# Two resnorm layers on one core: the hand-made order of every engine written anew, step by step, with a table of places per group

## The chip, the cores and the metric

The kernel runs on one core of one Trainium2 chip. The metric is the device time of one execution in microseconds (us), the median of several runs. Five instruction streams matter: PE (TensorE, matrix products), DVE (VectorE), ACT (ScalarE), POOL (GpSimd) and SP (SyncE, which only issues DMA transfers). Each stream is executed strictly in the order in which it was written; between streams there are semaphores.

## The reference, cut to what matters

`x` is 128 samples of 128 nodes by 512 features in float32, `adj` a 128 by 128 matrix. Layer 0 adds a graph convolution's maximum to `x` and normalizes; layer 1 is masked self-attention with 8 heads, a projection, an inner normalization with gamma and beta, a residual and an outer normalization.

```
# layer 0: one number per node is added to its 512 features
A   = adj @ x[b];  r = max(relu(A + b0), over the features)
x1  = layernorm(x[b] + r)
# layer 1
q, k, v = x1 @ w_qkv                      # 8 heads of 64
attn = softmax(where(adj == 0, -inf, q @ k.T / 8))
o    = (attn @ v) @ w_proj + b_proj
out  = layernorm(x1 + o + layernorm(o) * gamma + beta)
```

## The kernel before

The 128 samples go in 32 groups of 4. A group passes through a software pipeline: its layer 0 is computed while the group before it makes its queries, keys and values, its softmax runs while the next group's layer 0 runs, and its projection overlaps the scores of the group after it.

The products with `w_qkv` and `w_proj` must be close to float32, but are run in the format float32r on parts with fewer bits. So each operand is split into a high part, a low part and a difference (`split`, `split_high`, `split_d`, lines 290 to 308), and each product is twelve 128x512 matmuls: eight into one PSUM bank (`product`, lines 342 and 343) and four into another (`product_d`, line 350). ACT takes the first bank out (`dense_main`), DVE adds the second (`dense_rest`). A group has 16 such products: 8 for queries and keys of all four samples (`dense` 4 to 11), 4 for values (`dense` 0 to 3), 4 for the projection (`po`). Besides them PE does, for each sample, the convolution (`conv`, line 186, 2 matmuls), the scores (`scores`, "S", line 397, 16 matmuls of 64x128) and the weighting of the values (`attend`, "AV", line 477, 16 matmuls of 128x64).

The transposes of the normalized `x` and of the attention weights are not made on PE but by DMA: ACT copies the two 16-bit halves of each number apart (`x_halves`, `halves`), a DMA writes them to DRAM (`rowsx`, `rows`), and a transposing DMA brings them back (`xT`, `eT`). Only in the last group are the weights transposed by PE ("T", line 464).

Buffers that matter: PSUM pool `ps_1` has four banks for one-bank tiles (convolution, AV, most products), `ps_2` two double banks (scores, some products); attention weights `e` have 3 buffers, their transposes `eT` 2, the projected `o` 3, the residual `xb` 2, `xt` 4.

The order of all streams is written by the program itself. Lines 561 to 872 make a list `plan` of (place, function): a PE order is fixed by hand (`pair_order`, `dense_order`, `tail_order`, `pro_order`), each PE step gets a place by adding lengths, and every other step is placed at a distance from its PE step, taken from the table `O`, within limits. The same distances hold for all groups; the first group has its own (`pro`), the last group and the one before it have partly their own (`final`, `last`, `tail`). Several instructions of one engine, or of two, are one step: `split` is two DVE instructions, `residual_x` two POOL ones, `stats` one ACT and three to four POOL ones, `halves` an ACT copy and a DMA, `norm_2` an ACT instruction and the DMA of the output. The sorted list is then run under `tc.manual_schedule`, so its order is the order on each engine, and only the order: the place itself is not a time that anything waits for. At the start `warm` (line 261) puts 28 small matmuls with no use into PE's stream.

Of the kernel before, what the change touches and what calls it, by code (L numbers as in the profile page):

```python
# [10 lines left out]
I32 = mybir.dt.int32  # L11
# [13 lines left out]

@with_exitstack
def tile_adj_resnorm_d2(
# [12 lines left out]

# [20 lines left out]
    xraws, rows, ends, xs, c0s, rms, pa, mv0s, pts, hs = {}, {}, {}, {}, {}, {}, {}, {}, {}, {}  # L85
    pps, qkTs, vs, pscs, es, ppts, eTs = {}, {}, {}, {}, {}, {}, {}
    pavs, oTs, xbs, os, sums_of, norms = {}, {}, {}, {}, {}, {}

    def load_x(b):
        xt = xpool.tile([P, D], FP, tag="xt", name=f"xt_{b}")  # L90
        nc.sync.dma_start(xt, x[b])
        xs[b] = xt


# [7 lines left out]
    adjT_ps = ps_1.tile([P, P], FP, tag="ps1", name="adjT_ps")  # L102
    nc.tensor.transpose(adjT_ps, adj_sb, ident)
    adjT = const.tile([P, P], FP, name="adjT")
    nc.vector.tensor_copy(adjT, adjT_ps)

    mask = const.tile([P, P], FP, name="mask")
    nc.vector.tensor_scalar(mask, adj_sb, 0.0, MASKED, op0=ALU.is_equal, op1=ALU.mult)
# [5 lines left out]

# [5 lines left out]
    raws = {}  # L120
# [15 lines left out]
    def load_w(c):  # L136
        if c < KC:
            if c % 2 == 0:
                pair = work.tile([P, 2, D], FP, tag="e", bufs=3, name=f"wraw_{c}")
                raws[c], raws[c + 1] = pair[:, 0, :], pair[:, 1, :]  # L140
            nc.scalar.dma_start(raws[c], part(c)[0])
            return
        raws[c] = work.tile([P, D], FP, tag="o", bufs=3, name=f"wraw_{c}")
        nc.sync.dma_start(shaped(c, raws[c]), part(c)[0])

    def split_w(c):

        _, (dst_h, dst_l, dst_d) = part(c)
        raw = raws.pop(c)
        wh = work.tile([P, D], FP, tag="xh", name=f"wh_{c}")  # L150
        nc.vector.tensor_scalar(wh.bitcast(I32), raw.bitcast(I32), HIGH, None, op0=ALU.bitwise_and)
        nc.vector.tensor_tensor(raw, raw, wh, op=ALU.subtract)
        nc.vector.scalar_tensor_tensor(
            dst_d, shaped(c, raw), HALF, shaped(c, wh), op0=ALU.mult, op1=ALU.subtract,
        )
        hs["w", c] = dst_h, dst_l, wh, raw

    def split_w_rest(c):
        dst_h, dst_l, wh, raw = hs.pop(("w", c))
        nc.scalar.activation(dst_h, shaped(c, wh), AF.Copy, scale=HALF)  # L160
        nc.scalar.activation(dst_l, shaped(c, raw), AF.Copy, scale=HALF)

    def row(vec):
        return bass.AP(tensor=vec.tensor, offset=vec.offset, ap=[[0, P], [1, D]])

    gamma_sb = const.tile([P, D], FP, name="gamma_sb")
    bias_sb = const.tile([P, D], FP, name="bias_sb")
    beta_sb = const.tile([P, D], FP, name="beta_sb")
    nc.vector.memset(mhalf, -0.5)
    square = const.tile([P, D], mybir.dt.bfloat16, name="square")  # L170

    nc.scalar.activation(mhalf, mhalf, AF.Copy)

    def load_gamma():
        nc.sync.dma_start(gamma_sb, row(ln_gamma))
        nc.sync.dma_start(bias_sb, row(b_proj))
        nc.sync.dma_start(beta_sb, row(ln_beta))


    def conv(b):  # L180

        g, i = divmod(b, G)
        if i == 0:
            rms[g] = small.tile([P, G], FP, tag="rm", bufs=2, name=f"rm_{g}")
        pa[b] = ps_1.tile([P, D], FP, tag="ps1", name=f"pa_{b}")
        nc.tensor.matmul(pa[b], adjT, xs[b], start=True, stop=True)  # L186

    def conv_max(b):
        g, i = divmod(b, G)
        nc.vector.tensor_reduce(rms[g][:, i : i + 1], pa.pop(b), AX.X, ALU.max)  # L190

    def relu_0(b, n):

        g, i = divmod(b, G)
        r = rms[g][:, i : i + n]
        nc.gpsimd.tensor_scalar(r, r, b0_sb, 0.0, op0=ALU.add, op1=ALU.max)

    def add_0(b):
        g, i = divmod(b, G)
        if g not in mv0s:  # L200
            mv0s[g] = small.tile([P, G, 4], FP, tag="sum0", bufs=5, name=f"sum0_{g}")
        nc.scalar.activation(
            xs[b], xs[b], AF.Identity, bias=rms[g][:, i : i + 1], accum_out=mv0s[g][:, i, 0:1],
        )

    def stats_0(b):
        g, i = divmod(b, G)
        squares(xs[b], mv0s[g][:, i, :])

    def rstd_0(b, n):  # L210
        g, i = divmod(b, G)
        total, ssq, nmean, shift = (mv0s[g][:, i : i + n, k] for k in range(4))
# [3 lines left out]
        for k in range(n):  # L216
            norms[b + k, 0] = ssq[:, k : k + 1], nmean[:, k : k + 1]
            c0s[b + k] = ssq[:, k : k + 1], shift[:, k : k + 1]

    def shift_0(b, n):  # L220

        g, i = divmod(b, G)
        _, ssq, nmean, shift = (mv0s[g][:, i : i + n, k] for k in range(4))
        nc.gpsimd.tensor_tensor(shift, rms[g][:, i : i + n], ssq, op=ALU.mult)
        nc.gpsimd.tensor_tensor(shift, shift, nmean, op=ALU.add)

    def stats_x(b):

        g, i = divmod(b, G)
        if g not in mv0s:  # L230
            mv0s[g] = small.tile([P, G, 4], FP, tag="sum0", bufs=5, name=f"sum0_{g}")
        st = small.tile([P, 6], FP, tag="bnst", bufs=2, name=f"bnst_{b}")
        nc.vector.bn_stats(st, xs[b])
        nc.vector.bn_aggr(mv0s[g][:, i, 0:2], st)

    def rstd_x(b, n):

        g, i = divmod(b, G)
        var = mv0s[g][:, i : i + n, 1]
# [3 lines left out]
    def shift_x(b, n):  # L243

        g, i = divmod(b, G)
        mean, rstd, both, shift = (mv0s[g][:, i : i + n, k] for k in range(4))
        r = rms[g][:, i : i + n]
# [3 lines left out]
        for k in range(n):  # L251
            norms[b + k, 0] = c0s[b + k] = rstd[:, k : k + 1], shift[:, k : k + 1]

    def norm_0(b, vector=False):
        rstd, nm = norms.pop((b, 0))
        if vector:
            nc.vector.tensor_scalar(xs[b], xs[b], rstd, nm, op0=ALU.mult, op1=ALU.add)
            return
        nc.scalar.activation(xs[b], xs[b], AF.Identity, bias=nm, scale=rstd)  # L259

    def warm(n):

        spare = ps_2.tile([P, 2, D], FP, tag="ps2", name=f"spare_{n}")
# [3 lines left out]
    def transpose_x(b):  # L267
        g, i = divmod(b, G)
        pts[b] = ps_1.tile([P, KC, P], FP, tag="ps1", name=f"ptx_{b}")
        xt = xs[b]  # L270
# [3 lines left out]
    def x_halves(b):  # L274

        planes = work.tile([P, 2, D], U16, tag="xplanes", bufs=1, name=f"xplanes_{b}")
        nc.scalar.copy(planes, xs.pop(b).bitcast(U16).rearrange("p (m s) -> p s m", s=2))  # L277
        rows["x", b] = dram.tile([P, 2, D], U16, tag="rowsx", bufs=8, name=f"rowsx_{b}")
        nc.sync.dma_start(rows["x", b], planes)

    def crossbar_x(b):
# [5 lines left out]

    x_forms = [group.tile([P, KC, G, P], FR, name=f"x_{n}") for n in "hld"]

    def split(key, src, dsts):  # L290

        _, fl, _ = dsts
        xh = work.tile([P, KC, P], FP, tag="xh", name=f"xh_{key}")
        nc.vector.tensor_scalar(xh.bitcast(I32), src.bitcast(I32), HIGH, None, op0=ALU.bitwise_and)  # L294
        hs[key] = dsts, xh
        nc.vector.tensor_tensor(fl, src, xh, op=ALU.subtract)  # L296

    def split_high(key, gpsimd=False):
        (fh, _, _), xh = hs[key]
        if gpsimd:  # L300
            nc.gpsimd.tensor_scalar(fh, xh, 1.0 / HALF, None, op0=ALU.mult)
        else:
            nc.scalar.activation(fh, xh, AF.Copy, scale=1.0 / HALF)

    def split_d(key, gpsimd=False):
        (fh, fl, fd), _ = hs.pop(key)
        engine = nc.gpsimd if gpsimd else nc.vector
        engine.tensor_tensor(fd, fh.bitcast(FP), fl.bitcast(FP), op=ALU.subtract)  # L308

    def copy_x(b, vector):  # L310

        xraws[b] = work.tile([P, H, P], FP, tag="eT", bufs=2, name=f"xraw_{b}")[:, :KC, :]
# [5 lines left out]
    def product_v(b):  # L318

        pps["v", b] = pv = ps_1.tile([P, D], FP, tag="ps1", name=f"pv_{b}")  # L320
        for kc in range(KC):
            nc.tensor.matmul(pv, xraws[b][:, kc, :], raws[kc], start=(kc == 0), stop=(kc == KC - 1))

    def keep_v(b):
        nc.scalar.copy(dense_to(0, b), pps.pop(("v", b)))

    def split_x(b):

        split(b, pts.pop(b), [f[:, :, b % G, :] for f in x_forms])


    def product(key, two, terms):

        if two:
            pp = ps_2.tile([P, 2, D], FP, tag="ps2", name=f"pp_{key}")
            pm, pd = pp[:, 0, :], pp[:, 1, :]
        else:
            pm = ps_1.tile([P, D], FP, tag="ps1", name=f"pm_{key}")
            pd = ps_1.tile([P, D], FP, tag="ps1", name=f"pd_{key}")
# [4 lines left out]
        pps[key] = pm, pd  # L344
        ends[key] = terms

    def product_d(key):
        terms, pd = ends.pop(key), pps[key][1]
# [3 lines left out]
    def dense(g, j, two):  # L352


        parts = [*zip(x_forms, qkv_forms)]
        if j < G:
            product((g, j), two, lambda kc: [(f[:, kc, j, :], w[:, kc, 2 * D :]) for f, w in parts])
            return
        c, k = divmod(j - G, 2)
        cs = slice(k * D + c * P, k * D + (c + 1) * P)  # L360
        product(
            (g, j), two,
# [536 lines left out]
```

## Time and profile before

| what | before |
|---|---|
| time, median of 3 runs | 1974.43 us (1974.4 to 1975.56) |
| profiled span | 1969.2 us |
| PE busy | 1844.8 us (94%) |
| DVE busy | 1671.3 us (85%) |
| ACT busy | 1550.6 us (79%) |
| POOL busy | 1273.3 us (65%) |
| DMA traffic | 302.92 MB, mean 154 GB/s |

"Busy" is the time in which an engine had an instruction in execution, as a share of the span. Line numbers (L397 and so on) are those of the kernel before. In a timeline a row gives the start, the duration, the engine and the operation, and in brackets the idle time before it with what ended it. A matmul's duration reaches past the start of the next one, since they are pipelined; the distance between two starts is what a matmul costs.

### The profile page before, as it was taken

The page shows a single profiled execution, that of the slowest core. Times are in us where ns is not written, and L with a number is a line of the kernel's source. Part 1 is how long each engine was busy: PE and PEld are TensorE (multiplying, and loading weights), DVE is VectorE, ACT ScalarE, POOL GpSimd, SP SyncE. Part 2 cuts the span into 40 slices and gives each one's busy share as a digit, 9 for nine tenths or more (in the row PEclk, how much of TensorE's full clock was granted, in tenths as well). Part 3 has the DMA queues.
Part 4 walks back from the last instruction along what each step waited for, and adds up shares of the span by engine and source line. Part 5 has one row for each costly group of instructions (what it writes and reads, how often), then busy time and mean ns, then how long its engine had stood idle before and what let it go on. Part 6 is the DMA issues. An engine that isn't in the chain of part 4 may idle for free.

```text
span 1969.2 us, 33044 instructions
## 1 busy us (share of the span) xinstructions
PE 1844.8 (94%) x10569; PEld 1438.0 (73%) x10569; DVE 1671.3 (85%) x2585; ACT 1550.6 (79%) x3926; POOL 1273.3 (65%) x1935
## 2 busy tenths in 40 slices
PE   7799999999999999999999999999999999999995
PEld 4677777777777777777777777777777777777774
DVE  7678888888888888888888888888888888888885
ACT  4688878788878788878788878788778788778764
POOL 3156667666667666667666667666667666667667
PEclk9899999999999999999999999999999999999997
DMA  4356565666565666555666555665555665555641
GB/s 130 102 156 165 152 160 146 171 171 168 150 160 148 169 171 166 150 159 148 170 171 168 150 159 147 166 174 158 154 161 145 174 172 159 155 161 145 155 114 53
DMA packets 486141, 302.92 MB, mean 154 GB/s; under 512 B 399440, under 2 KB 403664, under 8 KB 485968
## 3 DMA queue, kind: packets, MB, share of 16 engines
q1 hardware_dynamic: 485104, 299.70, 57.5%
q8 instruction: 84, 1.38, 0.3%
q10 hardware_dynamic: 864, 1.12, 0.2%
q14 instruction: 89, 0.73, 0.1%
HBM read 72.16 MB, written 131.07 MB: 103 GB/s over the span
## 4 chain that ended last, share of the span: by engine, by line
PE 59%; POOL 14%; DVE 9%; ACT 7%; issue 5%; DMA 5%; POOLq 0%; ACTq 0%; SPq 0%; DVEq 0%
POOL x_d L308 5%; PE pav L477 4%; PE psc L397 4%; DMA eT<-rows 3%; PE pa L186 2%; POOL od L308 2%; ACT e L431 2%; POOL sum L536 2%; POOL xb L501 1%; DVE x_l L296 1%; DVE v L381 1%; DVE xh L294 1%; POOL xb L518 1%; POOL xb L500 1%; DVE o L523 1%
## 5 line engine op out<-in xcount | busy, mean ns | idle before, releaser
L431 ACT ACTIVATE e<-e,nmax 128x128 f32<-128x128 f32 x1016 | 393.1, 389 | 61.6 <-DVE nmax L422 61.6
L446 ACT COPY planes<-e 128x2048 uint16<-128x2048 uint16 x124 | 235.0, 1895 | 24.1 <-DVE e L440 21.6
L535 POOL TENSOR_SCALAR sum<-sum 128x1 f32<-128x1 f32 (+1 forms) x287 | 57.7, 201 | 284.7 <-ACT square L529 271.6
L529 ACT ACTIVATE square<-o,sum 128x512 bf16<-128x512 f32 x256 | 183.0, 715 | 63.7 <-DVE o L523 62.6
L501 POOL TENSOR_TENSOR xb<-xb,beta_sb 128x512 f32<-128x512 f32 x128 | 210.5, 1645 | 10.7
L308 POOL TENSOR_TENSOR x_d<-x_h,x_l 128x512 fp32r<-128x512 f32 x97 | 125.5, 1308 | 110.2 <-DVE x_l L296 51.6
L536 POOL TENSOR_TENSOR sum<-sum,mhalf 128x1 f32<-128x1 f32 (+1 forms) x287 | 180.1, 628 | 23.9
L431 ACT ACTIVATION_READ_ACCUMULATOR e<-e,nmax 128x1 f32 x1016 | 191.4, 188 | 0.0
L518 POOL TENSOR_TENSOR xb<-xb,o 128x512 f32<-128x512 f32 x125 | 175.2, 1401 | 4.9
L477 PE MATMUL pav<-eT,v 128*64 128x128 f32 x2048 | 140.7, 280 | 37.3 <-DMA eT<-rows 28.7
L548 DVE SCALAR_TENSOR_TENSOR o<-o,sum,gamma_sb 128x512 f32<-128x512 f32 x128 | 99.3, 776 | 75.4 <-POOL xb L518 71.9
L440 DVE TENSOR_TENSOR e<-e,sums 128x1024 f32<-128x1024 f32 x128 | 157.7, 1232 | 4.4
L477 PEld LDWEIGHTS pav<-eT,v 128*64 128x64 f32 x2048 | 110.8, 137 | 63.5 <-ACT square L529 19.9
L413 DVE SCALAR_TENSOR_TENSOR e<-psc,mask 128x1024 f32<-128x1024 f32 x127 | 152.0, 1217 | 3.4 <-ACT planes L446 2.7
L422 DVE TENSOR_REDUCE nmax<-e 128x8 f32<-128x1024 f32 x127 | 153.6, 1210 | 0.1
L259 ACT ACTIVATE xt<-xt,sum 128x512 f32<-128x512 f32 x127 | 102.4, 806 | 57.7 <-POOL sum L250 56.7
L556 ACT ACTIVATE o<-o,sum 128x512 f32<-128x512 f32 x128 | 103.2, 807 | 54.4 <-POOL sum L544 54.4
L397 PE MATMUL psc<-qkT 64*128 64x128 f32 x2048 | 142.6, 285 | 2.9 <-DVE qkT L381 2.6
L500 POOL TENSOR_SCALAR xb<-xb,sum 128x512 f32<-128x512 f32 x128 | 120.8, 944 | 34.2 <-DMA xb<-in_x_dram 34.0
L397 PEld LDWEIGHTS psc<-qkT 64*128 64x128 f32 x2048 | 124.1, 190 | 25.8 <-issue 21.6
L523 DVE SCALAR_TENSOR_TENSOR o<-o,sum,xb 128x512 f32<-128x512 f32 x128 | 132.5, 1035 | 10.8 <-POOL sum L536 0.9
L277 ACT COPY xplanes<-xt 128x1024 uint16<-128x1024 uint16 x124 | 129.7, 1046 | 6.2 <-DMA rowsx<-xplanes 2.4
(4668 smaller groups left out, 5611.1 us busy)
## 6 DMA issues: line engine op xcount, KB each, us to landing
rows<-planes SPq DMA_DIRECT2D x124, 512.0 KB, 3.4
xt<-in_x_dram SPq DMA_DIRECT2D x128, 256.0 KB, 3.0
xb<-in_x_dram SPq DMA_DIRECT2D x128, 256.0 KB, 2.9
out_dram<-o SPq DMA_DIRECT2D x128, 256.0 KB, 2.8
rowsx<-xplanes SPq DMA_DIRECT2D x124, 256.0 KB, 2.4
wraw<-in_L_gnn_w_qkv_dram SPq DMA_DIRECT2D x8, 256.0 KB, 3.0
xT<-rowsx SPq DMA_TRANSPOSE x124, 3.6
eT<-rows SPq DMA_TRANSPOSE x124, 4.7
```

What stands on the lines that cost most here:

```text
L308: engine.tensor_tensor(fd, fh.bitcast(FP), fl.bitcast(FP), op=ALU.subtract)
L397: nc.tensor.matmul(psc[:, s, hp, :], qkT[hs, hp, i, :], qkT[hs, KC + hp, i, :], start=not with_mask, stop=not with_mask or hp == HP - 1,)
L422: nc.vector.tensor_reduce(nmax, src, AX.X, ALU.max, negate=True)
L431: nc.scalar.activation(e[:, j, :], src[:, j, :], AF.Exp, bias=nmax[:, j : j + 1], scale=1.0 if src is e else scale, accum_out=sums[:, j : ...
L440: nc.vector.tensor_tensor(e, e, sums[:, :, None].to_broadcast([P, H, P]), op=ALU.mult)
L446: nc.scalar.copy(planes, e.rearrange("p h m -> p (h m)").bitcast(U16).rearrange("p (m s) -> p s m", s=2),)
L477: nc.tensor.matmul(pavs[b][s * HD : (s + 1) * HD, hp, :], v[:, h * HD : (h + 1) * HD], eT[:, s * HP + hp, :], start=True, stop=True,)
L501: nc.gpsimd.tensor_tensor(xbs[b], xbs[b], beta_sb, op=ALU.add)
L518: engine.tensor_tensor(xbs[b], xbs[b], os[b], op=ALU.add)
L523: nc.vector.scalar_tensor_tensor(os[b], in0, scalar, in1, op0=ALU.mult, op1=ALU.add, accum_out=s[:, 0:1],)
L529: nc.scalar.activation(square, x, AF.Square, bias=s[:, 0:1], scale=-float(D), accum_out=s[:, 1:2],)
L536: nc.gpsimd.tensor_tensor(s, s, mhalf[:, :n], op=ALU.pow)
```

## The change

Every step is now what one engine does at one time: `split_x` became `xmask` and `xsub`, `heads` became `omask` and `osub`, `weights` became `recip` and `wts`, `halves` became `pln` (ACT) and `row` (DMA), `residual_x` became `resx` and `resb`, `stats` became `sq1`/`sm1`/`st1` and `sq2`/`sm2`/`st2`, `norm_1` became `n1a` and `n1b`, `norm_2` became `norm2` and `out`, and a product's two halves (`dm` and `dd`, `po` and `pod`) are placed apart from each other and take their PSUM banks apart. Each step of each sample of a group has its own place in a table `STEADY`, group g's places being shifted by g times `PERIOD`. Groups 0 and 1 and groups 30 and 31 have tables of their own (`FIRST`, `LAST`), and the preparation of the weights has `SETUP`. The rules that held steps within limits are gone. The aim is that any step can be put anywhere in its engine's order, instead of moving with the steps it was bundled with.

What is computed, and by which instructions, stays the same, apart from these: the warming matmuls are gone (`'warm': []`), one first-group normalization moved from DVE to ACT, group 30's attention outputs go to ordinary tiles and no longer into the query and key weights' room, its residuals use the pool `xb` (2 buffers) instead of `xt` (4), and three pools of small tiles have more buffers.

```diff
+PERIOD = 54.43882
+STEADY = {
...
+    'conv': [-75.080, -64.352, -67.023, -70.602],
...
+    'xmask': [-47.658, -42.468, -38.679, -34.118],
+    'xsub': [-43.076, -38.349, -34.726, -32.646],
+    'xhigh': [-47.158, -38.788, -33.148, -33.668],
...
+    'dm': [3.754, 7.444, 16.569, 13.785, -22.455, -31.523, -27.895, -19.783, -26.082, -24.268, -29.709, -4.527],
+    'dd': [9.258, 19.289, 20.196, 11.065, -13.491, -8.148, -10.819, -9.055, -17.969, -15.305, -11.726, -2.714],
...
+    'rest': [12.301, 26.117, 23.001, 18.511, -5.215, -4.627, -1.871, -7.670, -15.367, -8.258, -10.618, -1.282],
+    'S': [0.000, 0.970, 6.474, 15.599],
+    'masked': [1.171, 4.033, 8.388, 26.711],
+    'rmax': [2.907, 10.127, 14.634, 29.080],
+    'exps': [6.022, 11.370, 22.296, 32.668],
+    'recip': [11.253, 17.788, 27.842, 35.882],
+    'wts': [12.895, 20.651, 37.253, 41.757],
+    'pln': [16.656, 25.869, 38.513, 45.479],
+    'row': [20.902, 29.660, 40.435, 47.401],
+    'cross': [24.543, 33.020, 43.404, 51.435],
+    'AV': [37.376, 47.198, 53.539, 64.603],
+    'omask': [39.660, 48.620, 56.741, 72.345],
+    'osub': [40.380, 50.401, 60.612, 73.544],
+    'ohigh': [44.959, 51.471, 59.941, 73.606],
+    'od': [48.023, 56.076, 68.476, 77.554],
+    'po': [48.098, 56.379, 66.410, 75.542],
+    'pod': [52.632, 60.006, 72.821, 94.480],
...
+    'sm1': [59.687, 67.486, 83.015, 100.647],
...
+    'n1a': [59.947, 79.246, 91.027, 101.796],
+    'n1b': [61.551, 82.391, 92.834, 105.448],
...
+    'out': [73.732, 100.113, 108.144, 131.860],
+}
+FIRST = [
...
+LAST = {
...
+SETUP = {
...
+    'warm': [],
+}
...
-            mv0s[g] = small.tile([P, G, 4], FP, tag="sum0", bufs=5, name=f"sum0_{g}")
+            mv0s[g] = small.tile([P, G, 4], FP, tag="sum0", bufs=7, name=f"sum0_{g}")
+            rms[g] = small.tile([P, G], FP, tag="rm", bufs=4, name=f"rm_{g}")
...
+    def bank(key, n, two):
...
+        if pps[key][n] is None:
+            pps[key][n] = ps_1.tile([P, D], FP, tag="ps1", name=f"p{'md'[n]}_{key}")
+        return pps[key][n]
...
-        n = b - (B - 2 * G)
...
+            n = b - (B - G)
...
+    for g in range(NG):
+        n = g - NG
+        group_plan(g, FIRST[g] if g < len(FIRST) else LAST[n] if -n <= len(LAST) else STEADY)
...
     plan.sort(key=lambda p: p[:2])
```

## The prediction, made before the changed kernel ran

> **What bounds the kernel now.** I read four views: the page's busy shares and slices, the windows of a middle group and of both ends, PE's timeline over a middle group, and the list of PE's waits.
>
> ```profile
> PE 1844.8 (94%) x10569; PEld 1438.0 (73%) x10569; DVE 1671.3 (85%) x2585; ACT 1550.6 (79%) x3926; POOL 1273.3 (65%) x1935
> ...
> PE   7799999999999999999999999999999999999995
> ...
> PEclk9899999999999999999999999999999999999997
> ```
>
> PE is in the nineties in every slice but the two ends, at full clock: the middle is PE's. Next the windows of one group (from the second AV of one round to that of the next), of the start up to the first scores, and of the end.
>
> ```profile
> core 0: us, PE busy (x) PEld busy (x) DVE busy (x) ACT busy (x) POOL busy (x), PEclk, DMA share, GB/s
> 1001.95:1061.02 59.07, 56.82 (x330) 44.41 (x328) 51.26 (x80) 48.31 (x123) 39.51 (x61) 1.00 0.63 157
> ...
> 0.00:62.00 62.00, 46.71 (x175) 30.59 (x175) 44.87 (x75) 33.35 (x58) 20.02 (x48) 0.94 0.39 116
> ...
> 1886.80:1969.20 82.40, 58.09 (x373) 44.64 (x372) 56.83 (x92) 42.06 (x120) 59.55 (x83) 0.86 0.25 74
> ```
>
> A group takes 59.07 us. The first scores start at 61.96 and those of group 31 at 1888.66, so the mean is 1826.7 / 31 = 58.9, with lighter groups at the start; between 291.39 and 1770.13, 25 groups took 59.15 each. The next busiest engine, DVE, has 7.8 us free in a group. What PE does with its 59.07 is in its timeline:
>
> ```profile
> 999.97 2.06 PE L397 MATMUL psc<-qkT 64*128 64x128 f32 x32
> 1001.95 1.09 PE L477 MATMUL pav<-eT,v 128*64 128x128 f32 x16
> 1002.98 0.50 PE L342 MATMUL pp_(16, 0)_10306<-w_h,x_h 128*128 128x512 f32 x1
> ...
> 1005.85 0.39 PE L342 MATMUL pm_('o', 60)_10338<-p_h,oh 128*128 128x512 f32 x1
> ...
> 1008.57 0.39 PE L342 MATMUL pm_(16, 1)_10370<-w_h,x_h 128*128 128x512 f32 x1
> ...
> 1011.29 0.39 PE L342 MATMUL pm_('o', 61)_10405<-p_h,oh 128*128 128x512 f32 x1
> ...
> 1014.10 1.16 PE L397 MATMUL psc<-qkT 64*128 64x128 f32 x16
> 1015.19 1.09 PE L477 MATMUL pav<-eT,v 128*64 128x128 f32 x16
> 1017.18 1.09 PE L477 MATMUL pav<-eT,v 128*64 128x128 f32 x16 [0.89 <-DMA eT<-rows]
> 1018.20 1.16 PE L397 MATMUL psc<-qkT 64*128 64x128 f32 x16
> ...
> 1032.86 1.20 PE L350 MATMUL pd_('o', 63)_10606<-p_d,od 128*128 128x512 f32 x4 [1.06 <-POOL od L308]
> ```
>
> From start to start: a product among products costs 2.72 (1005.85 to 1008.57). Before S a product costs 2.81, so the switch adds 0.09; a pair of S costs 1.98, an S before something else 1.09. AV costs 1.03, the product after it 2.87 (+0.15), the one after S 2.86 (1019.29 to 1022.15, +0.14), the one ahead of AV 2.94 (1055.07 to 1058.01, +0.22). Two convolutions take 1.31 (1039.68 to 1040.99) and the product after them 3.17 (+0.45).
>
> The sum without waits: 16 products, 43.5; [AV S S AV] = 0.22 + 1.03 + 1.98 + 1.03 + 0.15 = 4.4; [S AV AV S] = 0.09 + 1.09 + 1.10 + 1.02 + 1.09 + 0.14 = 4.5; two pairs of convolutions at 1.75, 3.5. Together 55.9. The other 3.1 us are waits: 0.89 for the transposed weights, 1.85 in and around `po` 63 (it takes 4.57 instead of 2.72) for `od`, 0.35 for a PSUM bank. In the list of waits these are the repeating ones:
>
> ```profile
> PE pav L477 <- DMA eT<-rows: 28.7, 26, 2.6
> ...
> PE pd_('o', 71)_11850 L350 <- POOL od L308: 1.6, 1, 1.6
> ```
>
> [...] PE is 56.8 of 59.07 busy, yet 3.1 us are waits and about 1.5 switches, partly inside "busy" durations. [...] the same `xh` from `xT` took 0.42 us at 1028.57 and 1.45 at 1030.23 while POOL worked; its mean is 0.735. [...] Here, after 3.78 us of idleness at 39.18, the next matmuls start 0.43 apart instead of 0.23.
>
> **The change part by part.** Work per engine stays: 44 PE steps of a group become the same matmuls in another order. Sorting the table by place modulo the period, PE's order is: S0 S1 po1 dm0 pod1 S2 dm1 dd0 AV3 dd3 po2 dm3 S3 dm2 pod2 dd1 dd2 po3 dm5 dm10 dm6 dm8 dm9 dm4 conv0 dm7 dd8 AV0 conv3 dd9 pod3 dd4 conv2 dd10 dd6 conv1 dd7 dd5 AV1 po0 dm11 dd11 pod0 AV2.
>
> *Waits removed.* AV0 stands 37.4 - 24.5 = 12.9 after its transposing DMA, which lands in 4.7 (page, median); AV1, AV2 and AV3 have 14.2, 10.1 and 13.2. The DMA wait goes. `od` stands 4.6, 3.9, 4.3 and 16.9 ahead of its `pod`, against 1.3 of its own time on POOL (0.7 on DVE): that wait goes too, since `pod` no longer follows `po` at once. Gain: up to 3.1 a group.
>
> *Switches added.* PE's small work was in four blocks between products, now it is in nine. At the costs above, [AV2 S0 S1] is 0.22 + 1.03 + 1.98 + 0.10 + 0.14 = 3.5; S2 and S3 alone 0.09 + 1.09 + 0.14 = 1.32 each; AV3 and AV1 alone 0.22 + 1.03 + 0.15 = 1.40 each; a lone convolution was never seen: between 0.88 (half a pair with its switch) and 1.1 (half a pair, the whole switch), I take 1.0; [AV0 conv3] 2.25. Sum with 16 products: 43.5 + 3.5 + 2.6 + 2.8 + 3.0 + 2.25 = 57.7. PE's own work rises by 1.8 a group. Splitting `dm` from `dd` costs nothing, since the matmuls have one shape. So at most 1.4 of 59.1 is left to gain.
>
> *Waits added.* The handover with least room to PE is xsub3 to dm5. PE reaches dm5 after six whole products, po3 (1.8), S0 S1 with switch (2.2), S2, AV3 and S3: 16.3 + 1.8 + 2.2 + 4.0 = 24.3 after S0. DVE has 29 instructions from masked0 to xsub3; at the undisturbed spacings of its timeline (1.17 for masked, 1.13 for rmax and wts, 0.45 for xmask, some 0.6 to 0.8 for the rest) they take 21.2 and start 1.2 after S0: 22.4. But eight of them are `xmask` and `xsub`, whose means are 0.735 and 0.914 against 0.42 and 0.69 undisturbed, with one `n1b` (1.035 against 0.75): 4 x 0.31 + 4 x 0.22 + 0.28 = 2.4, so 24.8. The wait is between 0 (no disturbance) and, if ACT and POOL handovers add to it, 1.5; I take 0.5. Behind dm5 on PE are all other main products of the next group, so this is paid in full. Other steps have room: rest11, which S0 waits for, stands 1.3 ahead of it.
>
> *The ends.* Their tables are free to differ, the work is the same. PE idles 15.3 us before the first scores, 11.9 in the next 59, 24.3 in the last 82. The warming matmuls fill 1.8 us on PE between two transposes; without them some products may run at half clock. I take 9 us of gain of these 51, with -5 to 20 as bounds.
>
> *Small edits* (more buffers of a few columns, one normalization moved, group 30's tiles) cost nothing: they touch 2 of 32 groups or instructions of 0.2 us beside PE's work.
>
> Sum: 59.1 - 57.7 - 0.5 = 0.9, taken as 0.8 with some further lag, over 30 groups: 24; with 9 at the ends, 33. 1974.4 - 33 = 1941.
>
> **The rivals.**
> *Cheap switches.* If much of the added switch cost lies in what follows only a long block, and DVE is never late, a group comes to 57.0: 2.1 x 30 = 63, ends 15: 1896. For it: DVE has 6 us to spare. Against it: every switch in the trace shows its cost, without a wait beside it.
> *DVE and POOL become the bound.* More handovers in one period, DVE at 51.3 + idle for each late step, and dm5 waits some 2.5: 60.2 a group, +32, ends -2: 2004, slower. For it: the DVE disturbances above, and steps on ACT and POOL that follow their source at once (exps1 after rmax1, n1a0 after sm1). Against it: 6 us of slack a group.
> *A wash.* The added waits just eat the 1.4: 1974.
>
> **How the numbers follow.** Forecast 0.46, cheap switches 0.23, wash 0.06, DVE-bound 0.25. Faster 0.69, within 0.2% 0.06, slower 0.25. The range reaches from the cheap case (1896, a little below) to near the slower one: 1893 to 1998.
>
> **What would show it.** In a middle group: right if the period is 58 to 58.6; if the product after a lone S or AV again costs 2.86 or more; if "DMA eT" has left PE's waits; and if dm5 (`pm_(g, 5)`) waits on DVE `x_l`. Wrong if PE's waits are of another kind (ACT, PSUM banks) or above 1.5 us a group, or if lone S and AV cost what they cost in pairs.

## The result and the profile after

The changed kernel takes 1891.43 us (median of 4 runs, 1887.61 to 1892.35) against 1974.41: ratio 0.9576, 95% interval 0.9559 to 0.9592. It is 83 us faster; 33 were forecast, and the time lies just under the range.

The page of the kernel after, its busy shares and slices:

```profile
PE 1842.2 (98%) x10541; PEld 1417.9 (75%) x10541; DVE 1597.0 (85%) x2584; ACT 1542.4 (82%) x3927; POOL 1387.2 (74%) x1935
...
PE   8999999999999999999999999999999999999995
...
PEclk9999999999999999999999999999999999999998
```

PE's busy time is what it was (1844.8 before); the span around it shrank. The windows of one group, of the start up to the first scores, and of the end (line numbers from here on are those of the kernel that ran):

```profile
core 0: us, PE busy (x) PEld busy (x) DVE busy (x) ACT busy (x) POOL busy (x), PEclk, DMA share, GB/s
1014.38:1071.59 57.21, 57.02 (x330) 44.18 (x329) 48.80 (x80) 47.91 (x123) 44.18 (x60) 1.00 0.60 166
0.00:49.00 49.00, 41.16 (x145) 26.47 (x145) 39.14 (x75) 30.60 (x54) 22.18 (x46) 1.00 0.50 147
1816.80:1885.80 69.00, 47.85 (x316) 36.11 (x312) 52.43 (x89) 40.49 (x120) 57.46 (x87) 0.91 0.20 59
```

A typical group takes 57.2 us instead of 59.07, and the profile has PE idle for 0.2 of them. Over 26 groups between 268.90 and 1763.93 the mean is 57.50 (before: 59.15). The start is 13 us shorter and never at half clock (granted clock 1.00 to 49.00, before 0.94 to 62.00).

So 1.65 x 30 = 50 of the 83 us come from the steady groups (24 forecast), and the remaining 33, by difference, from both ends with their lighter groups (9 forecast).

PE's timeline over part of that group (start, duration, operation):

```profile
1004.91 1.02 PE L486 MATMUL pa<-xt,adjT 128*128 128x512 f32 x2
1005.37 1.49 PE L676 MATMUL pd_(17, 7)_10807<-x_d,w_d 128*128 128x512 f32 x4
1006.70 1.07 PE L676 MATMUL pd_(17, 5)_10818<-x_d,w_d 128*128 128x512 f32 x4
...
1021.16 1.07 PE L676 MATMUL pd_('o', 65)_10991<-p_d,od 128*128 128x512 f32 x4
1022.16 1.16 PE L716 MATMUL psc<-qkT 64*128 64x128 f32 x16
1023.25 0.50 PE L670 MATMUL pm_(17, 1)_11024<-w_h,x_h 128*128 128x512 f32 x1
...
1025.20 1.10 PE L676 MATMUL pp_(17, 0)_10963<-w_d,x_d 128*128 128x512 f32 x4
1026.23 1.09 PE L802 MATMUL pav<-eT,v 128*64 128x128 f32 x16
1027.26 1.20 PE L676 MATMUL pd_(17, 3)_11065<-w_d,x_d 128*128 128x512 f32 x4
1028.29 0.39 PE L670 MATMUL pp_('o', 66)_11090<-p_h,oh 128*128 128x512 f32 x1
```

The distance from start to start is what a step costs (the first-half matmul at 1028.29 lasts 0.39, those behind it start 0.23 apart). A second half (`pd`, four matmuls) among products takes 0.91. Ahead of a lone S it takes 1.00, the S 1.09, and the first half after it 1.95 instead of 1.81: together 1.32 for the S, as forecast. Around the lone AV: 1.03, 1.03, 1.03, so AV costs 1.03 + 2 x 0.12 = 1.27, not 1.40. A lone convolution takes 0.46 plus 0.42 in the step behind it (1005.37 to 1006.70), 0.9, not 1.0.

### The profile page after: what moved, and what is told of

Its sections match the earlier page's. It is cut to its first block, busy times and chain, and to the rows that moved or that the text cites. A ratio compares the mean times of both kernels' runs of the same rounds, so it can differ in the third digit from the quotient of the medians.

```text
span 1885.8 us, 32740 instructions
## 1 busy us (share of the span) xinstructions
PE 1842.2 (98%) x10541; PEld 1417.9 (75%) x10541; DVE 1597.0 (85%) x2584; ACT 1542.4 (82%) x3927; POOL 1387.2 (74%) x1935
## 5 line engine op out<-in xcount | busy, mean ns | idle before, releaser
L862 POOL TENSOR_TENSOR xb<-xb,o 128x512 f32<-128x512 f32 x125 | 199.5, 1596 | 77.1 <-DVE o L865 74.7
L876 POOL TENSOR_SCALAR sum<-sum 128x1 f32<-128x1 f32 (+1 forms) x287 | 99.1, 345 | 207.1 <-ACT square L871 193.2
L877 POOL TENSOR_TENSOR sum<-sum,mhalf 128x1 f32<-128x1 f32 (+1 forms) x287 | 212.8, 742 | 23.9
L858 POOL TENSOR_TENSOR xb<-xb,beta_sb 128x512 f32<-128x512 f32 x128 | 180.4, 1409 | 2.8
L607 POOL TENSOR_TENSOR x_d<-x_h,x_l 128x512 fp32r<-128x512 f32 x97 | 141.1, 1456 | 11.3 <-DVE x_l L613 10.2
L761 DVE RECIPROCAL sums<-sums 128x8 f32<-128x8 f32 x128 | 24.6, 192 | 133.1 <-ACT e L755 133.1
L486 PE MATMUL pa<-xt,adjT 128*128 128x512 f32 x256 | 134.7, 613 | 0.4 <-DVE adjT L415 0.4
L855 POOL TENSOR_SCALAR xb<-xb,sum 128x512 f32<-128x512 f32 x128 | 100.7, 787 | 34.5 <-DMA xb<-in_x_dram 33.2
L865 DVE SCALAR_TENSOR_TENSOR o<-o,sum,xb 128x512 f32<-128x512 f32 x128 | 125.3, 979 | 0.6
```

What stands on the lines that cost most here:

```text
L607: engine.tensor_tensor(d, h.bitcast(FP), l.bitcast(FP), op=ALU.subtract)
L858: nc.gpsimd.tensor_tensor(xbs[b], xbs[b], beta_sb, op=ALU.add)
L862: engine.tensor_tensor(xbs[b], xbs[b], os[b], op=ALU.add)
L877: nc.gpsimd.tensor_tensor(s, s, mhalf[:, :n], op=ALU.pow)
```

## The experiments

Labels that begin with b are edits of the kernel before, with a of the kernel after. Each ratio is to the kernel before, in runs on the same chip.

**Take a repeating wait of PE out of the kernel before (b_pod, b_pod2, b_pod3).** The second half of `po` 3, which waits for `od`, comes one product later:

```diff
-            at(u + 1.87, product_d, ("o", b))
+            later = i == 3 and b < B - 2 * G
+            at(u + (4.71 if later else 1.87), product_d, ("o", b))
...
-            at(u + 2.8 + O["po_rest"][i], projected_rest, b)
+            at(u + (5.7 if later else 2.8 + O["po_rest"][i]), projected_rest, b)
-           'stats_1': [8.25, 13.1, 5.08, 3.38],
+           'stats_1': [8.25, 13.1, 5.08, 6.5],
```

> Kernel before, one edit: the second half of the fourth projection (product_d of po 3) no longer follows its first half at once but comes one product later, behind dense 4 of the next group. Theory A (a wait of PE for od is a pure loss, which a second half placed apart takes away, and a switch between two products costs nothing): period 59.15 - 1.85 = 57.3, so 30 x 1.85 = 55 us less: 1919 us, and 'pd <- POOL od' gone from PE's waits. Theory B (the wait only hides another one: DVE or POOL is late by as much elsewhere): another wait of PE grows in its place and the time stays above 1955 us.

Measured: 2041.25 us, ratio 1.0328 (1.0301 to 1.0354). Slower by 65 where theory A wanted 55 off. The timeline of b_pod on PE, DVE and POOL, where dense 4 follows:

```profile
1006.93 0.39 PE L343 MATMUL pm_('o', 59)_9983<-p_l,ol 128*128 128x512 f32 x1
1009.62 0.47 PE L342 MATMUL pp_(16, 4)_10018<-x_h,w_h 128*128 128x512 f32 x1 [2.30 <-POOL xb L500]
...
1011.56 0.63 PE L343 MATMUL pp_(16, 4)_10018<-x_l,w_l 128*128 128x512 f32 x1
1011.99 0.63 PE L342 MATMUL pp_(16, 4)_10018<-x_h,w_h 128*128 128x512 f32 x1
...
1005.75 1.44 DVE L294 TENSOR_SCALAR xh<-xT 128x512 int32<-128x512 int32 x1
1007.23 1.64 DVE L296 TENSOR_TENSOR x_l<-xT,xh 128x512 fp32r<-128x512 f32 x1
...
1005.61 1.30 POOL L308 TENSOR_TENSOR x_d<-x_h,x_l 128x512 fp32r<-128x512 f32 x1 [0.69 <-ACT x_h L303]
1006.86 1.46 POOL L308 TENSOR_TENSOR od<-oh,ol 128x512 fp32r<-128x512 f32 x1
1008.30 1.20 POOL L500 TENSOR_SCALAR xb<-xb,sum 128x512 f32<-128x512 f32 x1
```

The od wait is gone: with a product between the halves PE no longer stands for `od`. Instead it stands 2.30 us ahead of dense 4. The profile names L500, but b_pod3 (below) shows that this is the step that ended last, not the one waited for. After the wait the matmuls start 0.43 apart instead of 0.23: half clock. So a wait of 1.06 us was exchanged for one of 2.3 and, in most groups, half clock behind it, up to 1.6 more.

Theory B is right in kind: the od wait had hidden a second one.

To see what holds dense 4, b_pod2 moved `residual_x` of the fourth sample 5 us later:

> As b_pod (kernel before, second half of po 3 one product later), and POOL's residual work of the same sample (residual_x) moves from right behind od, beside DVE's last x_l, to 5 us later. Theory A (dense 4 waits for the last x_l, which POOL beside it stretches from 0.69 to 1.64 us; [...] the 2.3 us of b_pod cost another 1.7 at half clock): the wait falls to about 1.2, no half clock, 2.8 less in each of 30 groups: 1957 us. Theory B (the split is late by itself): the wait stays at 2 or more and the time within 15 us of 2041.

Measured: 2041.31 us, 1.033 (1.0305 to 1.0355), wait 2.32. The residual work beside `x_l` is the third sample's, so this run, though its time is theory B's, tells nothing of either. b_pod3 moved the right one (`'residual_x'` 5.33 to 11.0, `'residual_o'` 5.17 to 11.2):

> As b_pod, and the residual work on POOL that really stands behind od and beside DVE's last x_l (that of the third sample, residual_x with residual_o behind it) moves 6 us later; b_pod2 had moved another sample's. Theory A (that work stretches DVE's last x_l to 1.64 us and so holds dense 4[...]): the wait ahead of dense 4 falls from 2.3 to about 1.3, the half clock goes, 2.5 to 3 less a group: 1955 to 1965 us. Theory B (dense 4 is held by the whole chain of DVE's splits, of which the last microsecond is not POOL's): the wait stays near 2 and the time above 2025 us.

Measured: 2229.52 us, 1.1287 (1.1253 to 1.1322). Its timeline on DVE and PE, then on POOL, and one row of its list of PE's waits:

```profile
1023.53 1.45 DVE L294 TENSOR_SCALAR xh<-xT 128x512 int32<-128x512 int32 x1
1025.02 1.64 DVE L296 TENSOR_TENSOR x_l<-xT,xh 128x512 fp32r<-128x512 f32 x1
1026.58 0.68 DVE L523 SCALAR_TENSOR_TENSOR o<-pp_('o', 54)_9299,o 128x512 f32<-128x512 f32 x1
...
1027.41 0.47 PE L342 MATMUL pp_(15, 4)_9393<-x_h,w_h 128*128 128x512 f32 x1 [2.31 <-DVE o L523]
...
1035.13 0.96 POOL L500 TENSOR_SCALAR xb<-xb,sum 128x512 f32<-128x512 f32 x1 [3.49 <-DMA xb<-in_x_dram]
```

```profile
PE pd_(12, 8)_7628 L350 <- DVE qkT L381: 5.0, 1, 5.0
```

`x_l` still takes 1.64 and PE still waits 2.31, with no residual work near. Theory B holds: DVE's chain is late by itself. The step of it that PE waits for is the one behind the split, the addition of the second half of `po` 2 (L523), which the list names here. In the kernel it empties the double bank of `ps_2` that dense 4 takes. In the kernel before, b_pod, b_pod2 and b_pod3 alike dense 4 starts 0.15 us after it ends (here 1027.26 to 1027.41) and 0.75 after `x_l` does, since one follows the other at once. The last group of b_pod, where other steps stand between them, tells them apart:

```profile
1928.88 0.69 DVE L296 TENSOR_TENSOR x_l<-xT,xh 128x512 fp32r<-128x512 f32 x1
...
1931.89 0.68 DVE L523 SCALAR_TENSOR_TENSOR o<-pp_('o', 118)_19253,o 128x512 f32<-128x512 f32 x1
...
1932.72 0.47 PE L342 MATMUL pp_(31, 4)_19323<-x_h,w_h 128*128 128x512 f32 x1 [1.95 <-DVE o L523]
```

So PE waits for a PSUM bank, and the split delays it by standing ahead on DVE. (Dense 4 reads `x_l` too, but that is ready 0.6 us earlier.) The split is stretched there, to 1.44 and 1.64 us in b_pod and 1.45 and 1.64 in b_pod3 and in the kernel before, against 0.42 and 0.69 with no long POOL instruction beside it; each time `x_d` and `od` stand beside it on POOL. Neither L523 nor these two were moved by themselves, so that they are the cause isn't shown.

The 190 us on top have a cause of their own. On POOL the moved step now stands behind a residual that waits 3.49 us for its DMA; `norm_1` on DVE waits 6.55 us for it, and the second half of qk product 8 on PE another 3.4 to 5.5, once a group.

**Single waits at the start and end of the kernel before (b_keep, b_tail), and all three edits together (b_three).**

```diff
-         'keep': [-3.31, 7.03],
+         'keep': [-3.31, -2.0],
```

> Kernel before, one edit: the copy of v 1 of group 0 out of its PSUM bank (keep_v) is put early on ACT, so that the convolution at 39.18 need not wait 3.78 us for the bank. Theory A (the start's waits are pure losses, and the half clock after this one too, 1.1 to 1.3 us): first scores at 57 to 58 instead of 61.96, time 1969 to 1970 us. Theory B (the start is paced by loads and ACT): first scores within 1 us of 61.96, time unchanged.

```diff
-          'norm_2': [13.32, 18.89, 14.16, 15.4],
+          'norm_2': [13.32, 18.89, 17.0, 15.4],
```

> Kernel before, one edit: the last normalization of sample 122 (norm_2 of the third sample of group 30) moves on ACT from before the copies of the transposed weights of samples 126 and 127 to behind them, since it waits 5.68 us for POOL and PE's AV waits 3.03 us behind it. Theory A (order on ACT costs the tail these 3 us): 2 to 3 us less, 1971 to 1972 us. Theory B (the tail is paced by POOL's and DVE's residual work): unchanged within 1 us.

> Kernel before with the three edits together (second half of po 3 later, keep_v early, norm_2 of sample 122 later). Theory A (independent losses add up): 55 + 5 + 2.5 = 62 less, 1912 us. Theory B (they overlap or give way to other waits): above 1940 us.

Measured: b_keep 1975.74 us, 0.9999 (0.9983 to 1.0015), first scores at 62.10; b_tail 1978.37, 1.0005 (0.9989 to 1.002); b_three 2043.57, 1.034 (1.0295 to 1.0385). Theory B three times. In b_tail AV's wait for `eT` fell from 3.8 to 1.0, and another row of PE's waits rose from 2.1 by the same 2.8:

```profile
PE pm_('o', 125)_20013 L342 <- POOL w_h L301: 4.9, 1, 4.9
...
PE pav L477 <- ACT eT L468: 1.0, 3, 0.5
```

In b_tail dense 4 of the last group also waits longer, 3.1 instead of 0.7, but that wait differs from run to run (1.95 in b_pod, 4.0 in b_pod2). In b_keep the 3.8 us wait of the convolution went, and 1.7 and 1.8 us for DVE and 1.0 more for ACT came.

**Undo single parts of the kernel after (a_pod, a_pod2, a_bundle).**

```diff
-    'pod': [52.632, 60.006, 72.821, 94.480],
+    'pod': [48.099, 56.380, 68.477, 77.555],
```

> Kernel after, one edit: every second half of a projection goes back to the place right behind its first half (behind one more product for the fourth, whose od comes later), as in the kernel before. Theory A (that the halves stand apart is what takes the od wait off PE): the wait returns, 1 to 1.85 us a group, 1920 to 1945 us, with 'pd <- POOL od' among PE's waits. Theory B (the wait went because od is ready earlier: in the trace of after od ends 1.4, 1.1, 0.2 us before the first half of its product does): within 0.2% of 1891.

Measured: 1932.67 us, 0.9784 (0.9747 to 0.9821). The time is theory A's, the reason isn't: in the middle groups no second half waits for `od`. But this run can't bring that wait back. In the kernel before it stood at the fourth projection alone (`po` 63, 67, 71 and so on), and there the edit leaves the first half of a product between the two halves, as it does for the third. A group takes 58.82 us, and such a row shows where some of it goes:

```profile
1046.90 1.20 PE L676 MATMUL pp_(17, 0)_10968<-w_d,x_d 128*128 128x512 f32 x4 [0.62 <-ACT v L695]
```

My edit had left `prest`, which empties the second half's bank, where it was. So a_pod2 moved it too:

```diff
-    'prest': [53.745, 63.958, 78.638, 95.588],
+    'prest': [51.9681, 62.2271, 76.8401, 84.6451],
```

> As a_pod, and with DVE's step that empties the bank of the second half (prest) moved forward along with it, to right behind the step for the first half. Theory A (a_pod lost its 41 us because the second half's PSUM bank was held up to 17 us longer, until prest at its old place; the od wait was never there): most of the 41 us come back, 1891 to 1905 us. Theory B (the halves must stand apart on PE): it stays at 1920 to 1940 us.

Measured: 1910.96 us, 0.9671 (0.9656 to 0.9685), 58.03 a group. In ratios, half of the loss (0.0113 of 0.0208) came back and half stayed, with the 0.62 us wait still there. The time lies between the two theories: the bank's time matters, and so does where the halves stand. In the group looked at, PE spends 0.9 us more around that wait and 0.3 more around `pod` 3 than the kernel after does, and 0.5 less at a copy on ACT that comes up below (copy 6). Why ACT is late with `v` isn't shown.

```diff
-    'xmask': [-47.658, -42.468, -38.679, -34.118],
-    'xsub': [-43.076, -38.349, -34.726, -32.646],
+    'xmask': [-47.658, -42.468, -34.727, -34.118],
+    'xsub': [-47.6579, -42.4679, -34.726, -34.1179],
-    'osub': [40.380, 50.401, 60.612, 73.544],
+    'osub': [39.6601, 48.6201, 56.7411, 72.3451],
```

> Kernel after, one edit: DVE's two split instructions are bundled again, xmask with xsub and omask with osub directly one behind the other, in STEADY alone. Theory A (single steps, each with a place of its own, carry the gain): DVE waits for buffers and for PE at the bundled steps and PE for x_l or ol: +1 us a group or more, over 1920 us. Theory B (the order as a whole carries it, the cut between these two steps little): within 0.3% of 1891.

Measured: 1925.08 us, 0.9749 (0.9717 to 0.9782), 58.73 a group: theory A. Moving these steps by 0.7 to 4.6 us brings a wait of S in nearly every group, beside 0.47 ahead of `dm5` in the group looked at, which the list puts down to ACT's copy of `v` 2 out of its bank:

```profile
PE psc L716 <- DVE e L730: 13.1, 28, 0.5
```

This shows what bundling costs in an order made for single steps. What an order made for bundled ones would take wasn't tried.

**The tables of the ends (a_first1b, a_last1).** In one run group 1 takes `STEADY` for everything behind `norm0`; in the other group 30 takes `STEADY` throughout. (With `STEADY` throughout for group 1 as well, run a_first1, the streams deadlock: each waits for another, and there is no time.)

```diff
+EARLY = {**STEADY, **{k: FIRST[1][k] for k in [...]}}
...
-        group_plan(g, FIRST[g] if g < len(FIRST) else LAST[n] if -n <= len(LAST) else STEADY)
+        group_plan(g, (FIRST[g] if g != 1 else EARLY) if g < len(FIRST) else LAST[n] if -n <= len(LAST) else STEADY)
```

```diff
+        group_plan(g, FIRST[g] if g < 2 else LAST[n] if -n <= 1 else STEADY)
```

> Kernel after, one edit: group 1 uses the table STEADY for everything behind its first normalization, instead of its own table. Theory A (the own tables of the first groups carry a good part of the gain at the ends, as group 30's own table carried 15 us): 8 to 16 us slower, 1899 to 1907 us, with new PE waits between 49 and 165 us. Theory B (group 0's own table does it): within 3 us of 1891.

> Kernel after, one edit: group 30 uses the table STEADY instead of its own. Theory A (the own table of the next to last group carries half of the 12 us gained at the end): 4 to 10 us slower, 1895 to 1901 us. Theory B (the last group's table alone does it): within 2 us of 1891.

Measured: a_first1b 1908.3 us, 0.9665 (0.9648 to 0.9682); a_last1 1906.75, 0.9655 (0.9624 to 0.9687): 17 and 15 us slower than the kernel after, theory A in both, by more than its figures. The windows behind the first scores, of a_first1b and then of the kernel after:

```profile
51.00:165.00 114.00, 101.09 (x537) 75.99 (x534) 88.15 (x138) 85.74 (x221) 53.27 (x71) 0.94 0.53 141
```

```profile
49.00:163.00 114.00, 110.30 (x658) 84.19 (x658) 100.60 (x157) 95.00 (x250) 59.06 (x83) 1.00 0.64 162
```

With its own table PE does 9 us more of its work there and stays at full clock (1.00, against 0.94 with `STEADY`). With `STEADY` it waits 4.7 us for the split (in this run's list `pm_(1, 5)` for ACT `x_h`) and 2.9 ahead of S.

**A version that beats both (a_best, a_best2).** AV of the fourth sample goes to stand behind S of the third, and the last group's `v` 2 is finished earlier; a_best2 also moves ACT's copy of qk product 6.

```diff
-    'AV': [37.376, 47.198, 53.539, 64.603],
+    'AV': [37.376, 47.198, 53.539, 60.930],
...
-        'rest': [25.733, 28.770, 55.322, 28.687,
+        'rest': [25.733, 28.770, 51.950, 28.687,
...
-    'main': [9.110, 14.458, 21.811, 16.171, -10.671, -29.055, -11.156,
+    'main': [9.110, 14.458, 21.811, 16.171, -10.671, -29.055, -12.900,
```

> Kernel after, two edits: AV of the fourth sample moves forward on PE to stand right behind the scores S of the third (one switch into a product and one out of it less, 0.08 to 0.1 and 0.14 us), and in the last group DVE adds the second half of v 2 three steps earlier, which AV of sample 126 waits 2.6 us for. Theory A (PE's switches are paid in full at this floor): 0.2 x 30 + 2 = 8 us less, 1882 to 1885 us. Theory B (handovers have only some tenths of room, so any moved step makes a new wait or holds a bank longer): 1891 to 1905 us.

> As a_best (AV of the fourth sample behind S of the third; v 2 of the last group earlier), and one more: ACT's copy of the first half of qk product 6 (main 6) moves ahead of sq1 of the fourth sample, behind which it waits 2 us for DVE while PE's second half of 6 waits for it (0.19 in the list, 0.36 by the distance of the steps). Theory A (what stands between PE and its floor of 56.6 are such single places): period 57.0 to 56.65, 10 us less than a_best: 1863 to 1867 us. Theory B (another wait comes in its place): 1871 us or more.

Measured: a_best 1874.65 us, 0.9493 (0.9478 to 0.9507); a_best2 1865.32, 0.9435 (0.9417 to 0.9453). ACT's timeline in a_best shows what the last edit takes away, and a group's window in a_best2 what is left:

```profile
999.08 0.72 ACT L871 ACTIVATE square<-o,sum 128x512 bf16<-128x512 f32 x1 [1.97 <-DVE o L865]
...
999.80 0.80 ACT L913 ACTIVATE o<-o,sum 128x512 f32<-128x512 f32 x1
1000.50 0.57 ACT L695 ACTIVATE qkT<-pp_(17, 6)_10627 128x512 f32<-128x512 f32 x1
```

```profile
956.02:1012.50 56.48, 56.48 (x330) 44.38 (x328) 48.75 (x80) 47.91 (x124) 44.17 (x61) 1.00 0.62 167
```

Copy 6, whose product had long ended, stood behind a 1.97 us wait in ACT's queue. Without that PE is never idle in a typical group, which takes 56.48 us: the wait had cost 0.46 (56.94 before this edit). The switch taken away was worth 0.2 to 0.3 (57.2 to 56.94 in typical groups), as estimated; much of the rest of a_best's gain is that irregular waits of the kernel after (some of its groups take 58 us or more) went too: its mean is 57.03, against 57.50. Theory A held in both runs, by more than its figure in the first.

## Why the prediction was wrong, and where it was right

The direction and the kind of gain were right. Two sizes failed, in nearly equal parts: the switches in a group and the ends.

**Waits removed: right in sum, and for the reason given.** Some 2.5 us of waits a group went, as forecast (3.1 to 0.6 there; measured, what the means of 59.15 and 57.50 leave above PE's own work, 3.2 to 0.8). Neither the DMA nor the od wait is in PE's list for the middle groups of the kernel after. `od` of the fourth projection, the only one waited for, still ends 0.9 us after its first half in the kernel after (1.2 in the kernel before), so it is the distance to `pod` that takes the wait off PE, as b_pod showed too:

```profile
1039.19 1.30 POOL L607 TENSOR_TENSOR od<-oh,ol 128x512 fp32r<-128x512 f32 x1
1039.37 0.39 PE L671 MATMUL pm_('o', 67)_11187<-p_l,ol 128*128 128x512 f32 x1
1039.59 0.39 PE L670 MATMUL pm_(18, 5)_11214<-x_h,w_h 128*128 128x512 f32 x1
```

One reading was wrong. Of the 1.85 us "in and around" `po` 63 only 1.06 are the wait for `od`. 0.45 are the switch behind the convolutions, which the two pairs at 1.75 hold already, and 0.34 are dense 4's own wait for DVE: its start comes 1.26 after that of the second half (1032.86 to 1034.12) instead of 0.91. The second wait was in view there.

That the two waits could be booked as a pure gain was itself luck. In the kernel before the od wait couldn't be taken out alone (b_pod), since the chain on DVE that ends with the bank for dense 4 was as late. The view that says so was there and wasn't read, the page's chain of work of the kernel before:

```profile
PE 59%; POOL 14%; DVE 9%; ACT 7%; issue 5%; DMA 5%; POOLq 0%; ACTq 0%; SPq 0%; DVEq 0%
POOL x_d L308 5%; PE pav L477 4%; PE psc L397 4%; DMA eT<-rows 3%; PE pa L186 2%; POOL od L308 2%; ACT e L431 2%; POOL sum L536 2%; POOL xb L501 1%; DVE x_l L296 1%; DVE v L381 1%; DVE xh L294 1%; POOL xb L518 1%; POOL xb L500 1%; DVE o L52
```

PE is 94% busy but only 59% of the chain. This fits a loop through several engines with little room, and not PE with some waits on top. The same view of the kernel after follows only the last 4% of the span and can't be set beside it.

**Switches added: the first mis-sized term.** Forecast were 57.7 us of PE work a group, 1.8 more than before. It is 56.7, 0.8 more: 56.48 of a_best2 without any wait, and some 0.25 for the switch taken out there. I charged 0.22 ahead of every AV, read at one place. In the kernel after it is 0.09 to 0.12 in 88 of the 101 places in middle groups where AV follows a second half; in the kernel before it is 0.09 as well in 25 of 27 middle groups, and the group that I read is one of the other two. First the usual case, then the one read:

```profile
997.94 1.07 PE L350 MATMUL pd_(16, 9)_10216<-x_d,w_d 128*128 128x512 f32 x4
998.94 1.09 PE L477 MATMUL pav<-eT,v 128*64 128x128 f32 x16
...
1056.88 1.07 PE L350 MATMUL pd_(17, 9)_10838<-x_d,w_d 128*128 128x512 f32 x4
1058.01 1.09 PE L477 MATMUL pav<-eT,v 128*64 128x128 f32 x16
```

With four AV and four convolutions (0.9 instead of 1.0) this makes up nearly all of the difference, 1.0 x 30 = 30 us, of which waits 0.2 a group longer than forecast take 6 back.

**Waits added: the wrong place, about the right size.** dm5 doesn't wait in any middle group (0.5 forecast, 0.1 more as lag). PE waits instead 0.46 a group for copy 6 on ACT, and 0.3 in the mean for irregular ones. The calculation of DVE's lateness charged `xh` its old mean of 0.735 us; after the change it is 0.452, since none of the 124 takes over 1 us any more (29 did before). `x_l` stays at its mean (0.914 and 0.922).

**The ends: the second.** 9 forecast, 33 measured. I counted 51 us of idleness and took a fifth, without a step that gave the share. Replacing the own tables by `STEADY` costs 17 us in group 1 and 15 in group 30, so that the tables matter is shown. They are no shares of the 33, since the kernel before didn't use `STEADY` there. How the 13 us before the first scores divide is not: b_keep shows only that the waits there give way to each other. The warming matmuls were not tried by themselves; the kernel after is without them and at full clock (1.00) to 49 us.

**Rivals.** "Cheap switches" (57.0 a group, ends 15, 1896) came closest, its ends still half of what they were. The DVE-bound case did not occur, though a_bundle shows how little room the order on DVE has: steps moved by a few us there cost 34.

**Open:** how much of the last `x_l`'s lateness in the kernel before goes with the POOL work beside it and how much with the order, whether b_pod with L523 moved forward would gain, and what the small edits (more buffers, group 30's tiles) do by themselves.

## What to carry to other kernels

Before a wait is booked as a gain, look for what is late just behind it: read the chain across engines, not only the list of waits of the busiest one. Read a cost that is multiplied by many in more than one group. In an order with tenths of a microsecond of room, take a wait away by moving what is queued ahead of its source (copy 6), and move the step that frees the buffer along with the step that fills it. Give the first and last rounds of a pipeline their own order, and estimate them step by step, since at 2 of 32 groups each they held two fifths of this gain.

## What the hardware showed

**PE's clock behind a wait.** In b_pod, dense 4's first half, which takes 1.9 us at full clock behind a wait, took 3.1 to 3.5 in 18 of the groups with a wait near 2.3, and 2.3 to 2.4 in six more; one with 2.32 took 1.9. After 2.1 us it took 1.9 in three groups of b_pod, but 3.5 in one of b_pod2 and 3.0 in one of b_pod3. So the length of the wait alone doesn't tell which it is. Two neighbouring windows around dense 4 of b_pod's group 2, then two of group 4:

```profile
core 0: us, PE busy (x) PEld busy (x) DVE busy (x) ACT busy (x) POOL busy (x), PEclk, DMA share, GB/s
146.43:149.84 3.41, 2.60 (x10) 1.50 (x8) 3.38 (x4) 3.16 (x4) 2.70 (x3) 1.00 0.43 154
149.84:153.25 3.41, 1.90 (x8) 1.61 (x9) 3.41 (x6) 0.82 (x2) 3.25 (x5) 1.00 0.46 121
269.31:272.72 3.41, 1.08 (x5) 0.60 (x4) 3.38 (x5) 1.69 (x3) 3.33 (x4) 1.00 0.22 70
272.72:276.13 3.41, 3.41 (x10) 2.64 (x8) 3.41 (x6) 1.36 (x7) 3.25 (x5) 0.50 0.66 230
```

Group 2's wait of 2.32 us lies partly in either window (0.81 and 1.51), and both are at full clock; group 4's of 2.33 lies in the first alone, and the second is at half clock, though PE is busy throughout. In the kernel before, the trace has eight stretches at a granted clock of 0.50: four of 3.41 us, two of 6.83, one of 10.24 and one of 9.84 up to the end. In the 3.41 us ahead of each, at clock 1.00, PE was busy for 0 to 1.39. What limit or rule stands behind this isn't shown.

**DVE beside POOL.** In b_pod DVE's `xh` took 1.44 us; it began 0.14 after a POOL `x_d` of 1.30 and ended 0.28 after it. In b_pod3 it took 1.45 (0.13 and 0.28). In the kernel before, the 28 `xh` with `x_d` and `od` beside them on POOL took 1.23 to 1.50, each ending 0.28 or 0.29 after `x_d`; the 38 with no POOL instruction of over 0.7 us beside them took 0.41 to 0.43. `x_l` took 1.63 to 1.65 in the 28 cases with `od` and L500's `xb` beside it and 0.69 in the 66 with none. Beside POOL's L536 on `sum` neither was longer (0.42 and 0.69, 25 times each). What it is in the hardware isn't shown. In b_pod the stretched `xh` and `x_l` stand ahead of the step that PE waits for.
